# LayerNorm scaling with gamma in PSUM, and five gate operations moved from VectorE to GpSimd

## The chip, the cores and the metric

The kernel runs on one core of a Trainium2 chip. The metric is device time in microseconds (us) of one execution; lower is better. Engines are named as in the profile: PE (TensorE matmul), PEld (its weight loads), DVE (VectorE), ACT (ScalarE), POOL (GpSimd), SP (SyncE, which here only issues transfers). Line numbers such as L331 are those of the kernel before the change; the changed file numbers the same statements two or three higher.

## The reference

The program is two layers on images x of shape 32 x 128 x 56 x 56, all in fp32. Only the first layer's normalisation and gating matter here:

```python
x = depthwise_conv_7x7(input) + dw_bias            # 32 images, 128 channels, 56 x 56
x = transpose(x, (0, 2, 3, 1))                     # tokens: T = 32*56*56 = 100352, C = 128
x = (x - mean(x)) / sqrt(var(x) + 1e-6) * ln_gamma + ln_beta
logits = x @ Wg + bg                               # E = 8 experts
topv, topi = top_k(logits, 2)
wts = softmax(topv)                                # w0, w1
order = argsort(-wts[:, 0])                        # tokens by priority, for the experts' capacity
# each expert keeps its first CAP = 1.25*T/8 tokens: gelu(x@W1+b1)@W2+b2, weighted by wts
out = input + x_skip + layer_scale * moe_out
```

The second layer (coordinate attention and a 3 x 3 convolution) follows and is not touched.

## The kernel before

The program runs in stages, one after the other in time: the depthwise convolution (0 to 600 us), the LayerNorm and gating stage (600 to 1095), the routing, that is, the search for each expert's threshold (from 1093), the experts (to 3120) and the second layer (to the end). A scheduling layer orders the instructions of each engine when the program is built; on the chip each engine then goes through its list in order, and waits on semaphores.

The LayerNorm stage takes two images at a time, a pair, as 49 tokens on each of 128 partitions, and a pair in two units of 24 and 25 tokens per partition (`halves`). For each unit:

- `centre` (L293): SP loads the pair's channels into `lnyt` (two tiles). PE multiplies each token column by `proj`, which subtracts the mean and also forms the eight logits (L310), into PSUM tiles of three tokens each (`lnp`, eight tiles). ACT copies them to `cen` (L311, four tiles) and squares them for the variance: for the first unit of a pair ACT sums as well (L315), for the second it leaves squares in `sqs` (L317).
- `spread` (L319): for the second unit DVE sums the squares (L322). POOL turns sums into variances (L323) and raises them to the power -1/2 (L324), giving `rstd`.
- `normalise` (L326): DVE scales each token with one instruction (L331): `cen` times its `rstd`, times gamma, which lies in SBUF as `gamma_bc`, on all partitions. The result goes into `row`, the pair's tile `xn` of 49 rows of 137 numbers (128 channels, 8 gates, one number for the later expert). Two such tiles exist (`xp`, bufs 2). L333 scales the logits.
- Once a pair: `top` (L234) finds the two largest logits with a chain of dependent DVE operations on 392 elements (49 tokens x 8 experts), leaving one-hot masks `oh0` and `oh1`. `exp` (L254) runs on ACT. `gates` (L257) forms the weights w0 and w1 and from them five arrays of 392 elements, then SP sends the row tile to `acc_d` in DRAM with one transfer of 3356.5 KB (L276).

The stages are pipelined: the loop at L337 centres unit k, normalises unit k-2, and runs `top` or `gates` for pair (k-3)//2. In the built order a pair's `gates` stand on DVE between the scalings of the first and the second unit of the next pair, directly behind the sum L322. The order there is: 24 scalings (the first of which needs the row tile of the pair two before to have reached DRAM), L333, L261, L270, L262, L322, L263, a scaling, L264, a scaling, L265, L267, L268, a scaling, L269, L272, a scaling, L274, the other 21 scalings, L333, then `top` of the same pair, and the first scaling of the next pair just before the last mask of `top` (L248).

`prio` (L274) holds each token's priority for each chosen expert. Routing reads it with its first count (L447). POOL's queue holds in this stage L323 and L324 for each unit; behind the stage come its memset of `zr` (L628), which starts a zero fill of part of `acc_d` that ACT issues (L631), and the scaling of the experts' weights (L722).

Of the kernel before, what the change touches and what calls it, by code (L numbers as in the profile page):

```python
# [8 lines left out]
F32 = mybir.dt.float32  # L9
# [4 lines left out]
ALU = mybir.AluOpType  # L14
AX = mybir.AxisListType
PSUM = bass.MemoryType.PSUM
DRAM = bass.MemoryType.DRAM

N, C, H, W = 32, 128, 56, 56
HW = H * W  # L20
T = N * HW
E = 8
CAP = int(1.25 * T / E)
FF = 4 * C
P = 128
NT = T // P
NPAIR = N // 2
TPP = 2 * HW // P
# [14 lines left out]
def bc(ap, shape):  # L43
    return ap.to_broadcast(shape)
# [3 lines left out]
def moe_conv_then_coordatt_kernel(ctx: ExitStack, tc: tile.TileContext, a: dict, out: bass.AP):  # L48
    nc = tc.nc
# [14 lines left out]
    def load(name, shape, src, eng=None):  # L64
        t = const.tile(list(shape), F32, name=name)
        (eng or nc.sync).dma_start(t, src)
        return t
# [12 lines left out]
    gamma_bc = load("gamma_bc", [P, C], a["ln_gamma"].rearrange("c x -> x c").partition_broadcast(P))  # L80
# [20 lines left out]
    with ExitStack() as st:  # L101
# [3 lines left out]
        pp = st.enter_context(tc.tile_pool(name="dwp", bufs=8, space=PSUM))  # L105
# [44 lines left out]
        for q in range(NQ_):  # L150
# [6 lines left out]
            for i, (t0, offsets, least) in enumerate(PRODUCTS):  # L157
# [14 lines left out]
                for r in range(QC):  # L172
                    c = QC * q + r
                    if i == 0:
                        k = (c % 2) * (C // 2) + c // 2
# [15 lines left out]
    prio = prp.tile([P, E, NT], F32, name="prio")  # L191


    with ExitStack() as st:
# [2 lines left out]
        qp = st.enter_context(tc.tile_pool(name="lnq", bufs=1, reuse_waits="tile"))  # L197
        xp = st.enter_context(tc.tile_pool(name="lnx", bufs=2, reuse_waits="tile"))
        sp = st.enter_context(tc.tile_pool(name="lns", bufs=3, reuse_waits="tile"))
        pp = st.enter_context(tc.tile_pool(name="lnp", bufs=8, space=PSUM))  # L200
        halves = ((0, TPP // 2), (TPP // 2, TPP))
        U = TPP - TPP // 2
        NSQ = TPP // 2
# [11 lines left out]
        def over_tokens(x, n):  # L215
            return bc(x.unsqueeze(1), [P, n, E])

        def over_experts(x, n):
            return bc(x.unsqueeze(2), [P, n, E])

        class Pair:
# [2 lines left out]
            def __init__(self, i):  # L224
                self.i = i

            def tile(self, pool, tag, shape=None):
                return pool.tile(shape or [P, TPP], F32, tag=tag, name=f"{tag}{self.i}", bufs=2 if pool is xp else 1)

            def open(self):  # L230
                self.row = self.tile(xp, "xn", [P, TPP, RW])
# [2 lines left out]
            def top(self):  # L234

                l, n = self.l, TPP
                nc.vector.tensor_tensor(l, l, over_tokens(logit_c, n), ALU.add)
                t = self.tile(sp, "gt", [P, TPP, E])
                self.oh = [self.tile(sp, f"oh{k}", [P, TPP, E]) for k in range(2)]
                self.m = [self.tile(sp, f"m{k}") for k in range(2)]  # L240
                self.later, second = self.tile(sp, "later"), self.tile(sp, "second")
                for k in range(2):
                    nc.vector.tensor_reduce(self.m[k], l, AX.X, ALU.max)
                    nc.vector.tensor_tensor(t, l, over_experts(self.m[k], n), ALU.is_equal)
                    nc.vector.tensor_tensor(t, t, over_tokens(rank_e, n), ALU.mult)
                    mx = (self.later, second)[k]
                    nc.vector.tensor_reduce(mx, t, AX.X, ALU.max)
                    nc.vector.tensor_tensor(self.oh[k], over_tokens(rank_e, n), over_experts(mx, n), ALU.is_equal)  # L248
                    if k == 0:
                        nc.vector.scalar_tensor_tensor(l, self.oh[0], -3.0e38, l, ALU.mult, ALU.add)  # L250
                nc.vector.tensor_tensor(self.m[1], self.m[1], self.m[0], ALU.subtract)
                nc.vector.tensor_tensor(self.later, self.later, second, ALU.min)
# [3 lines left out]

            def gates(self):  # L257

                n, mx, w0, w1 = TPP, self.m[1], self.tile(sp, "w0"), self.tile(sp, "w1")
                t = self.tile(sp, "gt", [P, TPP, E])  # L260
                nc.vector.tensor_tensor(mx, mx, one_t, ALU.min)  # L261
                nc.vector.tensor_tensor(w0, mx, one_t, ALU.add)  # L262
                nc.vector.reciprocal(w0, w0)  # L263
                nc.vector.scalar_tensor_tensor(w0, w0, 0.5, one_t, ALU.max, ALU.min)  # L264
                nc.vector.tensor_tensor(w1, mx, w0, ALU.mult)  # L265
                row, oh = self.row, self.oh
                nc.vector.tensor_tensor(row[:, :, C : C + E], oh[0], over_experts(w0, n), ALU.mult)  # L267
                nc.vector.tensor_tensor(t, oh[1], over_experts(w1, n), ALU.mult)  # L268
                nc.vector.tensor_tensor(row[:, :, C : C + E], row[:, :, C : C + E], t, ALU.add)  # L269
                nc.vector.scalar_tensor_tensor(row[:, :, C + E : RW], self.later.unsqueeze(2), -1.0, all_e.unsqueeze(2),  # L270
                                               ALU.mult, ALU.add)
                nc.vector.tensor_tensor(oh[1], oh[0], oh[1], ALU.add)  # L272
                cols = slice(self.i * TPP, (self.i + 1) * TPP)
                nc.vector.tensor_tensor(prio[:, :, cols].rearrange("p e t -> p t e"), oh[1], over_experts(w0, n), ALU.mult)  # L274
                rows = slice(self.i * TPP * P, (self.i + 1) * TPP * P)
                nc.sync.dma_start(acc_d[rows, :].rearrange("(p j) c -> p j c", p=P), row)  # L276

# [2 lines left out]
        class Unit:  # L280
# [45 lines left out]
            def normalise(self):  # L326
                pair = pairs[self.i]
                if self.h == 0:
                    pair.open()
                for j in range(self.n):  # L330
                    nc.vector.scalar_tensor_tensor(pair.row[:, self.j0 + j, 0:C], self.cen[:, j, 0:C],  # L331
                                                   self.rstd[:, j : j + 1], gamma_bc, ALU.mult, ALU.mult)
                nc.vector.tensor_tensor(pair.l[:, self.j0 : self.j1, :], self.cen[:, :, C : C + E],  # L333
                                        over_experts(self.rstd, self.n), ALU.mult)

# [16 lines left out]
    with ExitStack() as st:  # L352
        rc = st.enter_context(tc.tile_pool(name="rc", bufs=1, reuse_waits="tile"))
        sp = st.enter_context(tc.tile_pool(name="rts", bufs=2, reuse_waits="tile"))
# [243 lines left out]
        xp = st.enter_context(tc.tile_pool(name="fx", bufs=1, reuse_waits="tile"))  # L598
# [30 lines left out]
        for k in range(4):  # L629
            r0, n = T1 + k * T // 4, T // 4 // P // BLK  # L630
# [227 lines left out]
    with ExitStack() as st:  # L858
        cp1 = st.enter_context(tc.tile_pool(name="cc", bufs=1, reuse_waits="tile"))
        xp = st.enter_context(tc.tile_pool(name="cx", bufs=2, reuse_waits="tile"))  # L860
        kp = st.enter_context(tc.tile_pool(name="ck", bufs=3, reuse_waits="tile"))
        sp = st.enter_context(tc.tile_pool(name="cs", bufs=2, reuse_waits="tile"))
# [23 lines left out]
        w0, w1, w2 = (wc[:, k] for k in range(3))  # L886
# [51 lines left out]
        for k in range(2):  # L938
            t = cp1.tile([C, H + 2, W + 2], F32, name=f"pad{k}")
# [196 lines left out]
```

## Time and profile before

| | us |
|---|---|
| median of three runs | 4329.18 |
| lowest and highest | 4310.08, 4334.66 |
| the profiled execution | 4323.54 |
| its span on the core | 4321.8 |
| DVE busy, of the span | 2571.0 (59%) |
| POOL busy, of the span | 2752.9 (64%) |
| PE busy, of the span | 3526.6 (82%) |
| L331, 784 scalings, busy | 213.5 |

The shares are averages over stages that differ; a stage is read from its own stretch. A line of the timeline gives the start (us from the span's start), the time that it took, engine, line, operation, out<-in, shapes, the number of instructions merged, and in brackets idle time in front and what ended it. DVE's records overlap: the next instruction starts up to some 0.1 us before the last has ended, so the cost of one is read from start to start. A line of a group gives after the bar the busy time in us and the mean duration of one in ns, and after the second bar the idle time in front. A line of the waits gives who waited for whom: us in total, times, the longest.

### The profile page before, as it was taken

Reading aid. Unit: us, or ns where it says so; the run is one execution under the profiler, and the core shown is the slowest. Engines: PE = TensorE matmul, PEld = TensorE weight load, DVE = VectorE, ACT = ScalarE, POOL = GpSimd, SP = SyncE. Lnnn points to the kernel's source line nnn. Section 1 sums busy time; section 2 is a strip of 40 time slices with the busy share of each in tenths; the row PEclk is TensorE's granted clock in tenths of the full one; section 3 lists DMA queues with packets and bytes.
Section 4 is the critical chain, followed back from the end, with each engine's and each line's share of the span. In section 5 each row is a group of like instructions: output and inputs, shape, how many; then the busy total and the mean of one; then the engine's idle time right before and its main releaser. Section 6 shows DMA issues by size and latency. Waiting matters only on the chain. (4 is left out here: it accounts for less than half of the span.)

```text
span 4321.8 us, 60777 instructions
## 1 busy us (share of the span) xinstructions
PE 3526.6 (82%) x21765; PEld 2018.7 (47%) x21765; DVE 2571.0 (59%) x5370; ACT 1447.6 (33%) x3123; POOL 2752.9 (64%) x2044
## 2 busy tenths in 40 slices
PE   7999979884169858778688668989669999999999
PEld 4555559884134434444344334434334444454444
DVE  4333329999748648775622112222268888888886
ACT  0000027664034424334344334545312333333332
POOL 5444414333057777576777467777779877788875
PEclk9999989786579879889799889999879999999999
DMA  9999985553982121111222122222265555555551
GB/s 183 179 186 191 188 179 222 245 239 166 327 267 51 51 61 43 48 44 49 54 56 56 45 59 57 56 56 57 60 226 163 193 182 176 166 192 182 184 163 73
DMA packets 678005, 580.92 MB, mean 134 GB/s; under 512 B 405848, under 2 KB 611184, under 8 KB 667248
## 3 DMA queue, kind: packets, MB, share of 16 engines
q1 hardware_dynamic: 411408, 319.81, 25.7%
q10 hardware_dynamic: 222816, 160.70, 14.1%
q0 software_dynamic: 43264, 94.64, 8.1%
q8 instruction: 187, 3.06, 0.3%
q14 instruction: 330, 2.70, 0.2%
HBM read 314.92 MB, written 260.09 MB: 133 GB/s over the span
## 5 line engine op out<-in xcount | busy, mean ns | idle before, releaser
L702 POOL DMA_INDIRECT acc_d<-yo,row x676 | 685.7, 1014 | 274.9 <-DMA acc_d<-yo,row 70.4
L1041 PE MATMUL pc<-v,wk 128*128 128x392 f32 x1920 | 705.5, 510 | 0.4 <-POOL v L1026 0.4
L661 PE MATMUL ph<-fxt,w 128*128 128x512 f32 (+1 forms) x1400 | 682.5, 631 | 0.5 <-ACT ht L662 0.5
L640 POOL DMA_INDIRECT xg_r<-acc_d,idx x556 | 557.4, 1003 | 183.9 <-issue 108.5
L669 PE MATMUL py<-ht,w 128*128 128x512 f32 (+1 forms) x1400 | 624.6, 589 | 0.0
L165 PE MATMUL acc<-xs,band 28*64 28x432 f32 (+2 forms) x11264 | 536.1, 527 | 51.8 <-issue 33.0
L662 ACT ACTIVATE ht<-ph,bias 128x512 f32<-128x512 f32 (+1 forms) x700 | 476.8, 682 | 248.9 <-PE ph L661 246.4
L1041 PEld LDWEIGHTS pc<-v,wk 128*128 128x128 f32 x1920 | 348.2, 191 | 308.5 <-issue 104.9
L165 PEld LDWEIGHTS acc<-xs,band 28*64 28x64 f32 x11264 | 311.2, 132 | 276.1 <-issue 182.9
L310 PE MATMUL lnps<-proj,lnyt 128*128 128x136 f32 x1568 | 364.7, 401 | 67.4 <-ACT sq L315 38.8
L661 PEld LDWEIGHTS ph<-fxt,w 128*128 128x128 f32 x1400 | 274.1, 207 | 279.3 <-issue 250.9
L310 PEld LDWEIGHTS lnps<-proj,lnyt 128*128 128x128 f32 x1568 | 350.9, 316 | 81.7 <-ACT sq L315 47.9
L669 PEld LDWEIGHTS py<-ht,w 128*128 128x128 f32 x1400 | 254.6, 190 | 261.1 <-issue 259.2
L1051 DVE SCALAR_TENSOR_TENSOR y<-pc,y 128x392 f32<-128x392 f32 x640 | 317.3, 553 | 14.9 <-PE pc L1041 14.9
L1021 POOL TENSOR_TENSOR d<-pad 128x3248 f32<-128x3248 f32 x32 | 228.0, 7125 | 151.8 <-DVE pad L1013 151.8
L958 POOL TENSOR_TENSOR cxn<-cxn,cx 128x896 f32<-128x896 f32 x112 | 267.3, 2395 | 75.6 <-DMA cxn<-acc_d 28.8
L696 DVE TENSOR_TENSOR ys<-pb,xg_r 128x512 f32<-128x512 f32 (+2 forms) x147 | 98.3, 671 | 341.3 <-PE pb L678 341.1
L181 DVE TENSOR_TENSOR yt<-acc,m 128x448 f32<-128x448 f32 x256 | 146.4, 620 | 260.3 <-PE acc L165 188.3
L671 ACT ACTIVATE fyt<-py,b 128x512 f32<-128x512 f32 (+1 forms) x175 | 119.6, 683 | 507.0 <-PE py L669 496.7
L653 DVE COPY fxt<-pt 128x512 f32<-128x512 f32 (+1 forms) x175 | 119.5, 683 | 241.7 <-PE pt L651 238.7
L693 ACT ACTIVATE yo<-xg_r,own 128x137 f32<-128x137 f32 (+1 forms) x568 | 194.3, 404 | 191.1 <-DVE own L689 128.3
L331 DVE SCALAR_TENSOR_TENSOR xn<-cen,rstd,gamma_bc 128x128 f32<-128x128 f32 x784 | 213.5, 340 | 47.2 <-POOL rstd L324 47.2
(243 smaller groups left out, 5035.4 us busy)
## 6 DMA issues: line engine op xcount, KB each, us to landing
acc_d<-xn SPq DMA_DIRECT2D x16, 3356.5 KB
acc_d<-yo ACTq DMA_DIRECT2D x4, 13426.0 KB
lnyt<-y_d SPq DMA_DIRECT2D x16, 3136.0 KB
x<-in_x SPq DMA_DIRECT2D x16, 3136.0 KB
cxn<-acc_d SPq DMA_DIRECT2D x112, 448.0 KB
cx<-acc_d SPq DMA_DIRECT2D x112, 448.0 KB
out<-y ACTq DMA_DIRECT2D x64, 784.0 KB
xt<-in_x ACTq DMA_DIRECT2D x64, 392.0 KB
```

The source lines that it names most:

```text
L165: nc.tensor.matmul(acc[r][half * M : (half + 1) * M, :, lo:hi], lhsT=band[rows, t0 + o - least, 1 - par : 1 - par + M], rhs=xs[i][rows, ha ...
L310: nc.tensor.matmul(ps[:, j, :], lhsT=yf[:, self.j0 + g + j, :], rhs=proj, start=True, stop=True)
L331: nc.vector.scalar_tensor_tensor(pair.row[:, self.j0 + j, 0:C], self.cen[:, j, 0:C], self.rstd[:, j : j + 1], gamma_bc, ALU.mult, ALU.mult)
L640: d = nc.gpsimd.indirect_dma_start(out=xg[0:n, k, :], out_offset=None, in_=acc_d[0:T1, :], in_offset=bass.IndirectOffsetOnAxis(ap=idx[0][0 ...
L661: nc.tensor.matmul(ph[:, 0:N_], lhsT=w[0][:, f * P : (f + 1) * P], rhs=xt[:, 0:N_], start=True, stop=True)
L662: nc.scalar.activation(ht[:, f, 0:N_], ph[:, 0:N_], AF.Gelu, bias=w[2][:, f : f + 1])
L669: nc.tensor.matmul(py[:, 0:N_], lhsT=w2[:, f, :], rhs=ht[:, f, 0:N_], start=(f == 0), stop=(f == NF - 1))
L702: d = nc.gpsimd.indirect_dma_start(out=acc_d[:, :], out_offset=bass.IndirectOffsetOnAxis(ap=row[0:n, k : k + 1], axis=0), in_=yo[0:n, k, : ...
L958: nc.gpsimd.tensor_tensor(xn, xn, x2, ALU.add)
L1021: nc.gpsimd.tensor_tensor(d, high, low, ALU.subtract)
L1041: nc.tensor.matmul(m[k], lhsT=wk[k][:, dw, :], rhs=v[:, k, rows, dw : dw + W], start=(dw == 0), stop=(dw == 2))
L1051: nc.vector.scalar_tensor_tensor(r[x], m[k], f, r[y_], ALU.mult, ALU.add)
```

## The change

Gamma is copied once into a PSUM tile, and the scaling reads it there. For it the PSUM pool of the products has seven tiles instead of eight. In `gates`, five operations on 392 elements are issued on POOL instead of DVE: the two products with w0 and w1 (L267, L268), their sum into the row (L269), the sum of the masks (L272) and the product for `prio` (L274). They work in place in the masks, without the tile `gt`, in a new order, and the masks and the weights have two tiles each.

```diff
-        pp = st.enter_context(tc.tile_pool(name="lnp", bufs=8, space=PSUM))
+        pp = st.enter_context(tc.tile_pool(name="lnp", bufs=7, space=PSUM))
+        gp = st.enter_context(tc.tile_pool(name="lng", bufs=1, space=PSUM))
+        gamma_ps = gp.tile([P, C], F32, name="gamma_ps")
+        nc.vector.tensor_copy(gamma_ps, gamma_bc)
...
-                self.oh = [self.tile(sp, f"oh{k}", [P, TPP, E]) for k in range(2)]
+                self.oh = [self.tile(sp, f"oh{k}", [P, TPP, E], 2) for k in range(2)]
...
-                n, mx, w0, w1 = TPP, self.m[1], self.tile(sp, "w0"), self.tile(sp, "w1")
-                t = self.tile(sp, "gt", [P, TPP, E])
+                n, mx, w0, w1 = TPP, self.m[1], self.tile(sp, "w0", None, 2), self.tile(sp, "w1", None, 2)
...
-                nc.vector.tensor_tensor(row[:, :, C : C + E], oh[0], over_experts(w0, n), ALU.mult)
-                nc.vector.tensor_tensor(t, oh[1], over_experts(w1, n), ALU.mult)
-                nc.vector.tensor_tensor(row[:, :, C : C + E], row[:, :, C : C + E], t, ALU.add)
                 nc.vector.scalar_tensor_tensor(row[:, :, C + E : RW], self.later.unsqueeze(2), -1.0, all_e.unsqueeze(2),
                                                ALU.mult, ALU.add)
-                nc.vector.tensor_tensor(oh[1], oh[0], oh[1], ALU.add)
+                nc.gpsimd.tensor_tensor(row[:, :, C : C + E], oh[0], over_experts(w0, n), ALU.mult)
+                nc.gpsimd.tensor_tensor(oh[0], oh[0], oh[1], ALU.add)
                 cols = slice(self.i * TPP, (self.i + 1) * TPP)
-                nc.vector.tensor_tensor(prio[:, :, cols].rearrange("p e t -> p t e"), oh[1], over_experts(w0, n), ALU.mult)
+                nc.gpsimd.tensor_tensor(prio[:, :, cols].rearrange("p e t -> p t e"), oh[0], over_experts(w0, n), ALU.mult)
+                nc.gpsimd.tensor_tensor(oh[1], oh[1], over_experts(w1, n), ALU.mult)
+                nc.gpsimd.tensor_tensor(row[:, :, C : C + E], row[:, :, C : C + E], oh[1], ALU.add)
...
-                                                   self.rstd[:, j : j + 1], gamma_bc, ALU.mult, ALU.mult)
+                                                   self.rstd[:, j : j + 1], gamma_ps, ALU.mult, ALU.mult)
```

More of the change, by code (lines that the diff above doesn't have):

```diff
@@ L225, in __init__, with tile @@
                 self.i = i
-            def tile(self, pool, tag, shape=None):
-                return pool.tile(shape or [P, TPP], F32, tag=tag, name=f"{tag}{self.i}", bufs=2 if pool is xp else 1)
+            def tile(self, pool, tag, shape=None, bufs=1):
+                return pool.tile(shape or [P, TPP], F32, tag=tag, name=f"{tag}{self.i}", bufs=2 if pool is xp else bufs)
             def open(self):
```

## The prediction

> **What bounds the kernel now.** I read the page's engine slices first (the change sits in slices 7 to 10, 600 to 1095 us), then the busy time by stretch. In the stretch 700 to 1000 us, columns after the window are PE, PEld, DVE, ACT, POOL busy time, granted clock, DMA share, GB/s:
>
> ```profile
> 650.00:700.00 50.00, 50.00 (x229) 50.00 (x229) 44.39 (x130) 40.22 (x182) 22.54 (x9) 1.00 0.50 197
> 700.00:1000.00 300.00, 258.39 (x1097) 246.13 (x1097) 296.35 (x845) 200.55 (x831) 118.50 (x45) 0.83 0.60 243
> ```
> ```profile
> ACT cen L311 <- DVE lgs L333: 92.2, 21, 6.9
> ```
>
> DVE works 296 of 300 us. PE leads only in the start-up (50 of 50 us), and the list of waits (third line) has ACT waiting for DVE. So a pair of images costs what DVE spends on it, which the DVE timeline shows:
>
> ```profile
> 814.54 0.34 DVE L331 SCALAR_TENSOR_TENSOR xn<-cen,rstd,gamma_bc 128x128 f32<-128x128 f32 x1
> ...
> 822.07 3.48 DVE L322 TENSOR_REDUCE var<-sqs 128x25 f32<-128x3200 f32 x1
> 825.46 0.46 DVE L263 RECIPROCAL w<-w 128x49 f32<-128x49 f32 x1
> ...
> 827.75 0.55 DVE L269 TENSOR_TENSOR xn<-xn,gt 128x392 f32<-128x392 f32 x1
> ...
> 842.00 0.34 DVE L331 SCALAR_TENSOR_TENSOR xn<-cen,rstd,gamma_bc 128x128 f32<-128x128 f32 x1
> ```
>
> The first scaling of a pair starts at 814.54 and of the next at 842.00: a period of 27.46 us. Call the end of L322 (825.46) the mark. The second thing to see: the first scaling writes a row tile of which there are two, so it must wait until the row of the pair two before is in DRAM. Here are POOL, SP, and the DMA share after the same mark:
>
> ```profile
> 825.64 0.21 POOL L323 TENSOR_SCALAR var<-var 128x25 f32<-128x25 f32 x1 [13.00 <-DVE var L322]
> 825.94 4.31 POOL L324 TENSOR_TENSOR rstd<-var,mhalf 128x25 f32<-128x25 f32 x1
> ```
> ```profile
> 828.33 0.33 SPq L276 DMA_DIRECT2D acc_d<-xn  x1
> 837.27 0.36 SPq L298 DMA_DIRECT2D lnyt<-y_d  x1
> ```
> ```profile
> 828.30:829.20 0.90, 0.90 (x6) 0.90 (x5) 0.90 (x3) 0.84 (x6) 0.90 (x1) 0.50 0.48 209
> 829.20:837.40 8.20, 7.59 (x35) 7.19 (x33) 8.06 (x27) 5.93 (x28) 4.61 (x3) 0.85 0.93 396
> 837.40:838.30 0.90, 0.90 (x5) 0.90 (x5) 0.87 (x2) 0.90 (x4) 0.90 (x1) 1.00 0.43 74
> ```
>
> The row leaves at 828.33, 0.03 us after L269 ends, and its packets end at 837.33; 842.00 is when its tile is wanted. There are under five microseconds to spare, and no wait shows. POOL spends 4.31 us on a power right behind the mark.
>
> **The change, part by part.**
>
> *Five operations leave DVE.* From start to start L267, L268, L269, L272 take 0.48 us each and L274 0.66: 2.57 us a pair.
>
> *gamma in PSUM.* A scaling of 128 elements takes 0.262 us from start to start now. The nearest row with one PSUM and one SBUF tensor and a per-partition scalar is L966: a 512 and a 384 together take 1.18 us (3921.42 to 3922.60). At 1.04 us per 1000 elements (3136 in 3.33 us at L1012, 392 in 0.47 at L1047) that leaves 0.123 us fixed, so 128 cost 0.257: 49 x 0.005 = 0.2 us a pair less. Bounds: -0.2, and +2.9 if what a per-partition scalar adds from SBUF (0.129 fixed against 0.069 of the 49 elements of L251, which pitch at 0.120) came once more with PSUM, 49 x 0.06; I take -0.2, as L966 is the nearest. [...] The copy into PSUM runs once, while DVE waits 47.2 us for the first rstd; were that cover gone it would be one copy, under 0.3 us.
>
> *Seven PSUM tiles for the products, not eight.* Hidden by ACT's waiting for DVE. In the start-up, where PE leads, three products less in flight (3 x 0.22 us): 0 to 0.7 us, once.
>
> *The five operations join POOL's queue.* In the built order each pair's five stand behind L323 and L324 of the unit just reduced:
>
> ```
> L325 var9_1 [waits DVE]   L326 rstd9_1   L271 xn7   L272 oh07   L274 prio   L275 oh17   L276 xn7
> ```
>
> (numbers of the changed file, two or three higher). So they start not when w0 is ready but when the power ends: 0.18 + 0.22 + 0.08 + 4.31 + 0.08 = 4.87 us after the mark. What is queued behind them is the next unit's L323, which ACT releases 8.3 us after the mark and which is wanted most of a period later: free. Their price comes from POOL's products of two SBUF tensors:
>
> ```profile
> L958 POOL TENSOR_TENSOR cxn<-cxn,cx 128x896 f32<-128x896 f32 x112 | 267.3, 2395 | 75.6 <-DMA cxn<-acc_d 28.8 <-PE pc L1041 18.8 <-issue 14.2
> ...
> L141 POOL TENSOR_TENSOR xs<-xt 128x1792 f32<-128x1792 f32 x32 | 101.5, 3172 | 32.6 <-DMA xt<-in_x 20.8 <-DMA y_d<-yt 11.4 <-POOL band L140 0.3
> ...
> L722 POOL TENSOR_TENSOR w<-w,ls_bc 128x512 f32<-128x512 f32 x8 | 10.2, 1276 | 39.2 <-PE ph L661 15.6 <-DVE ys L696 6.8 <-DVE lo_r L516 6.6
> ```
>
> L958's 896 elements take 2.094 (its median; the mean of 2.395 holds collisions) and L722's 512 take 1.276: 2.13 ns an element, so 392 take 1.02 us. Five, with four gaps of 0.08: 5.4 us. Low: L141's 1.77 ns an element, 0.69 each, 3.8 us. High: strides, as between L1031 (2.03 us) and L1026 (1.65) of one size, a factor of 1.23: 6.6 us.
>
> *The two engines meet.* These rows show a product on POOL and DVE operations with two SBUF inputs excluding each other:
>
> ```profile
> 1086.68 2.66 POOL L722 TENSOR_TENSOR w<-w,ls_bc 128x512 f32<-128x512 f32 x2 [3.92 <-DMA w<-in_W]
> 1086.79 1.27 DVE L262 TENSOR_TENSOR w<-m,one_t 128x49 f32<-128x49 f32 x1
> ```
>
> L262 (0.20 elsewhere) is held until POOL's first product is done. L966 and L1051, with one input in PSUM, keep their pace beside L1021 on POOL (3919 to 3926), so the scalings from PSUM should leave POOL free. They end 7.0 us after the mark: two or three of the five run undisturbed, the others meet top()'s chain. I add 1.0 us to POOL's five (two waits of about 0.5), from 0 to 3.0 (two waits of 1.6, as L323 shows at 1.81 against 0.21), and 2.2 us to DVE's chain (it waits out two products that began first, 1.02 each, and a gap; 0 to 5.1 for five). [...]
>
> *The row leaves later.* From the first scaling of pair p+1 to that of p+2 now runs: 10.92 to the mark, less 24 x 0.005: 10.8; queue and power 4.87; five operations 6.4; SP 0.03; issue to last packet 0.83 + 8.96 (mean of the eleven steady transfers in the trace's packets, 8.16 to 10.03) = 9.79; landing to the waiting engine 0.76 (the first matmul of the stage, 617.58 to 618.34). Sum 32.65 us. The load lnyt, which SP issues right behind, runs after it: lnyt0 and lnyt1, issued 0.45 us apart, moved in turn.
>
> DVE's own work is 27.46 - 2.57 - 0.2 + 2.2 = 26.9 us, inside 32.65. So the saving hides behind a new wait of 5.8 us: DVE's first scaling waits for the DMA. Per pair 32.65 - 27.46 = +5.2 us, for the fourteen pairs 2 to 15: +72.7. Bounds by the five operations (3.8 to 9.6): 30.05 to 35.85, +36 to +117; by the transfer (8.16 to 10.03) another -11 to +15.
>
> *The tail.* After pair 15 starts, DVE saves pair 14's 2.57 and the 1.07 + 0.8 us that L722 held L262 and L614; the last three operations to prio take 3.3 us on POOL against 3.2 now. Routing starts 4.3 us sooner, but the zero fill of acc_d, behind five gates and two L722 in POOL's queue, 0.5 us later. I take -2 (-4.3 to +0.5).
>
> Sum: +71 us. The profiled execution took 4323.54 (span 4321.8 plus 1.7), so 4394; the median of the three runs is 5.6 above it, so 4400.
>
> **The rivals.**
>
> *Faster.* The row still lands in time and DVE's work sets the period: 24.7 us without meeting, -2.76 x 15 - 2 = -43, 4286. It decides once five operations take under 1.2 us (26.25 + 1.2 = 27.46). For it: before has spare time at that wait. Against: 0.24 us each, a third of the lowest row.
>
> *About the same.* Operations at 0.5 us and transfers of 8.2 us: 28.0, +8 us, 4337. No row is that fast.
>
> *POOL starved.* Each of the five is kept out by DVE's chain like L323: 5.4 + 5 x 1.6 = 13.4, period 39.6, +168, 4497; with three of them +115, 4444. Against: the chain's dependent gaps let POOL in.
>
> *PSUM slows the scaling.* At the upper bound, 0.06 us each, 24 of them lie in the loop: +1.5 a pair, +21, 4421. Against: L966.
>
> **How the numbers follow.** The row wait as summed 0.70 (4360 to 4430); PSUM slow on top 0.08; starved 0.11; about the same 0.05; faster 0.06. Range 4352 to 4440, leaving out both ends. 0.5% (22 us) is about what a measurement tells from no change, as the three runs span 25. Faster 0.06, same 0.05, slower 0.89.
>
> **What would show it.** Right: idle time on DVE before the scaling, released by the DMA acc_d<-xn, some 5 us in fourteen places; the row leaving about 11 us after L322's end; POOL's five at about 1 us each; scalings at 0.257 us; DVE busy about 27 of 32.6 us. Wrong: no such wait, or POOL's five ahead of the power, or far under a microsecond.

## The result, and the profile after

The changed kernel takes 4383.64 us (median of six runs, 4372.19 to 4394.32) against 4323.16 before (six runs, 4310.08 to 4334.66): a ratio of 1.0150 with a 95% interval of 1.0129 to 1.0172, so 60 us slower. The forecast was 4400, the range 4352 to 4440. The profiled execution took 4379.09, with a span of 4377.3.

The time lies where it was expected. From the first product of the LayerNorm stage to the first count of the routing it was 474.4 us before and is 528.1 now: +53.7. The rest of the program differs by a few microseconds in both directions: in the profiled executions the stage starts 6.2 us later after the change, and what follows it is 4.2 us shorter.

The busy time of the stretch from 700 to 1000 us, whose columns are those of the same view before (window, its length, PE, PEld, DVE, ACT, POOL, granted clock, DMA share, GB/s):

```profile
700.00:1000.00 300.00, 225.83 (x981) 218.30 (x981) 242.27 (x678) 178.06 (x735) 139.83 (x89) 0.82 0.54 215
```

No engine is full any more. VectorE worked 296 of 300 us before and works 242 now, and nothing else took its place at the top. That is the sign of a wait that everything shares, and the list of waits over the whole stage (who waited for whom: us in total, times, longest) names it in the second line here:

```profile
ACT cen L313 <- DVE lgs L335: 145.4, 12, 13.4
...
DVE xn L333 <- DMA acc_d<-xn: 73.4, 14, 6.3
```

Fourteen waits of 5.2 us in the mean; the line was not there before. ACT's wait for VectorE grew with it (102.9 us in 24 waits before, over the whole stage) and is its echo: in the kernels below that have no such wait it is at 89 to 103 us again. One turn of the loop, on VectorE:

```profile
822.13 0.45 DVE L265 RECIPROCAL w<-w 128x49 f32<-128x49 f32 x1
...
829.13 0.87 DVE L335 TENSOR_TENSOR lgs<-cen,rstd 128x200 f32<-128x200 f32 x1
830.04 1.12 DVE L240 TENSOR_TENSOR lgs<-lgs,logit_c 128x392 f32<-128x392 f32 x1
...
842.52 0.35 DVE L333 SCALAR_TENSOR_TENSOR xn<-cen,rstd,gamma_ps 128x128 f32<-128x128 f32 x1 [5.29 <-DMA acc_d<-xn]
...
853.35 0.45 DVE L265 RECIPROCAL w<-w 128x49 f32<-128x49 f32 x1
```

on POOL:

```profile
822.60 4.31 POOL L326 TENSOR_TENSOR rstd<-var,mhalf 128x25 f32<-128x25 f32 x1
826.87 0.87 POOL L271 TENSOR_TENSOR xn<-oh,w 128x392 f32<-128x392 f32 x1
827.82 1.01 POOL L272 TENSOR_TENSOR oh<-oh,oh 128x392 f32<-128x392 f32 x1
828.91 0.87 POOL L274 TENSOR_TENSOR prio<-oh,w 128x392 f32<-128x392 f32 x1
829.74 0.99 POOL L275 TENSOR_TENSOR oh<-oh,w 128x392 f32<-128x392 f32 x1
830.81 1.20 POOL L276 TENSOR_TENSOR xn<-xn,oh 128x392 f32<-128x392 f32 x1
```

and on SP's queue:

```profile
832.03 0.33 SPq L278 DMA_DIRECT2D acc_d<-xn  x1
834.33 0.36 SPq L300 DMA_DIRECT2D lnyt<-y_d  x1
```

Read them in this order. The reciprocal starts at the mark (822.13, then 853.35: a period of 31.22 us). The power stands ahead of the five operations, the row leaves at 832.03, 9.90 us after the mark (2.87 before), its packets run from 832.87 to 842.06, and the scaling that wants the tile has been standing for 5.29 us when it starts at 842.52. The two lines at 829.13 and 830.04 are operations held by POOL's products: 0.87 and 1.12 us where they take 0.35 and 0.57 otherwise.

### The profile page after: what moved, and what is told of

It reads as the page before. It is cut to its first block, busy times and chain, and to the rows that moved or that the text cites. A ratio compares the mean times of both kernels' runs of the same rounds, so it can differ in the third digit from the quotient of the medians.

```text
span 4377.3 us, 60783 instructions
## 1 busy us (share of the span) xinstructions
PE 3522.8 (80%) x21765; PEld 2026.0 (46%) x21765; DVE 2550.2 (58%) x5291; ACT 1447.5 (33%) x3123; POOL 2803.4 (64%) x2124
## 5 line engine op out<-in xcount | busy, mean ns | idle before, releaser
L165 PE MATMUL acc<-xs,band 28*64 28x432 f32 (+1 forms) x11264 | 536.0, 528 | 58.3 <-issue 41.2
L1053 DVE SCALAR_TENSOR_TENSOR y<-pc,y 128x392 f32<-128x392 f32 x640 | 317.4, 554 | 11.2 <-PE pc L1043 11.2
L333 DVE SCALAR_TENSOR_TENSOR xn<-cen,rstd,gamma_ps 128x128 f32<-128x128 f32 x784 | 208.5, 339 | 120.5 <-DMA acc_d<-xn 73.4
## 6 DMA issues: line engine op xcount, KB each, us to landing
acc_d<-xn SPq DMA_DIRECT2D x16, 3356.5 KB
```

Of the source, the lines that this page charges most:

```text
L165: nc.tensor.matmul(acc[r][half * M : (half + 1) * M, :, lo:hi], lhsT=band[rows, t0 + o - least, 1 - par : 1 - par + M], rhs=xs[i][rows, ha ...
L1053: nc.vector.scalar_tensor_tensor(r[x], m[k], f, r[y_], ALU.mult, ALU.add)
```

## The experiments

Theory: the period is the row tile's loop, and the price is the late row. Rivals: GpSimd and VectorE exclude each other, and that is what is paid; GpSimd's own work; gamma in PSUM.

The scheduling layer answers most edits with another order on VectorE, which would change the loop too. So the kernels below (unless said otherwise) get VectorE's order of the changed kernel by force, with edges that order and need no semaphore:

```diff
+        for x, y in zip(rows, rows[1:]):      # rows: VectorE's instructions in the wanted order
+            tc.add_manual_dep(y.ins, x.ins.name, mybir.DependencyInfo(mybir.DependencyClass.NoSync, ...))
```

In the first four kernels below this list costs 2 us once, between the second and the third mark (24.2 to 24.4 us against 22.2 in the changed kernel).

Eight of the eleven kernels ran on chips on which the kernel before takes 4872 to 4886 us instead of 4323 (the three others, need later with four tiles, load a pair sooner and w1 first, where it takes 4318). No profile of the kernel before was taken there; in the profiles of the edited kernels the LayerNorm stage is as long as their edits alone account for, and the time from the routing to the end is 490 to 570 us longer. So times are compared by their ratio to the kernel before on the same chip, and the expectations, written with the first chip's 4323, are to be read as differences from it. "Period" is the mean of the thirteen intervals between the third and the sixteenth mark; "stage" reaches from the first product to the first count.

| kernel | period, us | stage, us | ratio to before, 95% interval |
|---|---|---|---|
| before | 27.45 | 474.4 | |
| the changed kernel | 31.27 | 528.1 | 1.0150, 1.0129 to 1.0172 |
| gamma alone | 27.26 | 476.9 | 1.0014, 0.9992 to 1.0035 |
| five operations alone | 34.81 | 578.3 | 1.0235, 1.0194 to 1.0276 |
| two operations for prio | 26.22 | 462.2 | 0.9973, 0.9948 to 0.9998 |
| five ahead of the power | 26.92 | 470.9 | 1.0024, 1.0006 to 1.0042 |
| need later | 31.83 | 542.0 | 1.0129, 1.0082 to 1.0175 |
| need later, four tiles | 27.68 | 483.2 | 1.0043, 1.0021 to 1.0065 |
| prio product last | 30.12 | 514.6 | 1.0086, 1.0056 to 1.0116 |
| load later | 31.11 | 528.0 | a single execution |
| load later, a pair sooner | 30.74 | 523.0 | a single execution |
| balanced | 25.31 | 451.3 | 0.9946, 0.9920 to 0.9971 |
| balanced, w1 first | 24.74 | 443.8 | 0.9923, 0.9896 to 0.9951 |

### Gamma alone

```diff
-                self.rstd[:, j : j + 1], gamma_bc, ALU.mult, ALU.mult)
+                self.rstd[:, j : j + 1], gamma_ps, ALU.mult, ALU.mult)
```

with seven PSUM tiles for the products, and the gate operations where they were.

> Gamma in PSUM alone; the five gate operations stay on VectorE, and VectorE's order is held as it was before. Theory (the row leaves late and VectorE waits for it): nothing in this part touches the row, so no wait for the transfer; a scaling every 0.258 us instead of 0.262 is 0.2 us a pair, about -3 us in all, 4320, no difference that can be measured. Rival (a scaling from PSUM is dearer): up to +0.06 us each, 49 a pair with VectorE the bound, +2.9 us a pair, +44 us, 4367.

The period is 27.26 us, 0.19 less than before; the forecast's term was 0.2. VectorE's timeline of this kernel:

```profile
822.89 6.02 DVE L341 SCALAR_TENSOR_TENSOR xn<-cen,rstd,gamma_ps 128x128 f32<-128x128 f32 x23
```

23 scalings from 822.89 to the next instruction at 828.83 are 0.258 us each, where one with gamma in SBUF took 0.262: PSUM is no dearer here. What the part does cost is the start-up: the first mark comes 0.9 us later and the interval from it to the second is 1.3 us longer (18.3 against 17.0). The kernel with eight PSUM tiles (the next one) does not show these 2.2 us, and all with seven do.

### The five operations alone

```diff
+                nc.gpsimd.tensor_tensor(...)          # the five, as in the change
-                self.rstd[:, j : j + 1], gamma_ps, ALU.mult, ALU.mult)
+                self.rstd[:, j : j + 1], gamma_bc, ALU.mult, ALU.mult)
```

> The five operations on GpSimd alone; gamma stays in SBUF, and VectorE's order is held as in the changed kernel. Theory: the row still leaves behind the power and the five operations, so the wait is there, and longer: the scalings that run beside the five now read two SBUF tensors and keep GpSimd out, up to the 1.6 us for each that L323 showed at its worst, and are held by it in turn. The period goes from 31.2 us to between 32 and 39; I take 34, +39 us against the changed kernel, about 4423. Rival (where gamma lies does not matter to GpSimd): the five take 5.1 us as in the changed kernel, period 31.2 to 31.4, 4384 to 4387.

34.81 us: the theory's number (34), not the rival's (31.2). POOL's timeline and VectorE's:

```profile
840.18 3.44 POOL L273 TENSOR_TENSOR xn<-oh,w 128x392 f32<-128x392 f32 x1
843.70 1.23 POOL L274 TENSOR_TENSOR oh<-oh,oh 128x392 f32<-128x392 f32 x1
```
```profile
837.81 4.80 DVE L336 SCALAR_TENSOR_TENSOR xn<-cen,rstd,gamma_bc 128x128 f32<-128x128 f32 x18
842.54 0.35 DVE L338 TENSOR_TENSOR lgs<-cen,rstd 128x200 f32<-128x200 f32 x1
842.92 1.12 DVE L239 TENSOR_TENSOR lgs<-lgs,logit_c 128x392 f32<-128x392 f32 x1
...
859.16 0.35 DVE L336 SCALAR_TENSOR_TENSOR xn<-cen,rstd,gamma_bc 128x128 f32<-128x128 f32 x1 [7.78 <-DMA acc_d<-xn]
```

The first product takes 3.44 us instead of 0.87: it ends at 843.62, 0.7 us after the train of scalings and the scaling of the logits behind it (842.89), while the scalings keep their pace (4.73 us for 18, 0.263 each). So a train of operations with two SBUF inputs kept GpSimd out almost until it ended. The kernel before has it too, on a shorter operation: the variance L323, 0.21 us otherwise, takes 1.81 us from 833.75 and ends at 835.56, just behind the logits' scaling that closes VectorE's train (835.49). So gamma in PSUM is worth 3.5 us a pair (34.81 against 31.27) to the five operations, as they stand; both parts of the change belong together.

### Two operations for prio

```diff
                 nc.vector ... row = oh0*w0; gt = oh1*w1; row += gt     # as before
-                nc.vector.tensor_tensor(oh[1], oh[0], oh[1], ALU.add)
+                nc.gpsimd.tensor_tensor(oh[1], oh[0], oh[1], ALU.add)
-                nc.vector.tensor_tensor(prio..., oh[1], over_experts(w0, n), ALU.mult)
+                nc.gpsimd.tensor_tensor(prio..., oh[1], over_experts(w0, n), ALU.mult)
```

> Gamma in PSUM; of the five, only the sum of the masks and the product for prio go to GpSimd, the three that the row needs stay on VectorE, whose order is else held. Theory: the row leaves 2.9 us after the mark again, and row tile's loop is 10.8 + 2.9 + 0.8 + 9.0 to 10.0 + 0.5 = 24 to 25 us; VectorE's own work is 27.46 - 0.2 - 1.14 = 26.1 us and sets the period: -1.3 us a pair, about -20 us, 4303, and no wait for the transfer. Rival (the engines exclude each other, so that what VectorE is spared comes back as holding): two operations of 1 us hold VectorE for up to 2 us, period 26.1 to 28.1, 4303 to 4333, in the main no change.

The period is 26.22 (forecast 26.1), and no wait for the transfer remains. The stretch from 700 to 1000 us, and POOL:

```profile
700.00:1000.00 300.00, 263.12 (x1142) 254.13 (x1142) 295.08 (x861) 210.47 (x876) 129.87 (x72) 0.88 0.64 259
```
```profile
837.05 1.02 POOL L281 TENSOR_TENSOR oh<-oh,oh 128x392 f32<-128x392 f32 x1
838.15 0.88 POOL L283 TENSOR_TENSOR prio<-oh,w 128x392 f32<-128x392 f32 x1
```

VectorE is full again (295 of 300 us) and saves 1.04 of the 1.14 us against gamma alone (27.26), beside two products of GpSimd that meet only scalings from PSUM. At most 0.1 us came back as holding. The ratio, 0.9973, is less than the -20 us expected, 0.9954: the thirteen periods are 16.0 us shorter, but the start-up is 4.7 us longer (PSUM tiles and list), and the stage is left with 12.2.

### The five ahead of the power

```diff
+        behind = [(units[2 * q + 5].up, pairs[q].last) for q in range(NPAIR - 2)]   # variance behind the fifth
```

> The changed kernel with the five operations ahead of the power (and the variance) of the unit just reduced in GpSimd's queue; VectorE's order is held. Theory: the five start when w0 is ready, about 1.0 us after the mark instead of 4.7; the row leaves 3.7 us sooner, and the loop is 31.2 - 3.7 = 27.5 us (up to 28.3 with the slower transfers), so the wait falls from some 5.5 us to 1 to 2, and the time to about that of before: 4323 to 4335. Rival (contention of GpSimd and VectorE is what the changed kernel pays): the same five operations meet the same engine, period 31.2, 4384.

```profile
832.50 0.87 POOL L276 TENSOR_TENSOR xn<-oh,w 128x392 f32<-128x392 f32 x1 [13.35 <-DVE w L271]
...
836.32 0.99 POOL L281 TENSOR_TENSOR xn<-xn,oh 128x392 f32<-128x392 f32 x1
...
837.69 4.32 POOL L331 TENSOR_TENSOR rstd<-var,mhalf 128x25 f32<-128x25 f32 x1
```
```profile
832.59 0.84 DVE L272 TENSOR_TENSOR w<-m,w 128x49 f32<-128x49 f32 x1
...
847.70 0.35 DVE L339 SCALAR_TENSOR_TENSOR xn<-cen,rstd,gamma_ps 128x128 f32<-128x128 f32 x1 [1.45 <-DMA acc_d<-xn]
```

The same instructions in another order on one queue, and the wait falls from 5.2 us in the mean to 1.5 and the period by 4.35 us, to less than the 27.5 expected. The rival of contention, which had 31.2, is out as the cause of the period. (The ratio, 1.0024, is some 15 us above what the stage's -3.5 us would give; the difference lies outside this stage and its cause is open.)

### The need later, and what took the wait's place

```diff
-  24 scalings of the first unit, their logits, the sum of squares (mark), w, 25 scalings of the second
+  12 scalings of the first unit, the sum of squares (mark), w, the other 12, their logits, 25 scalings of the second
```

This is VectorE's list before and after. 12 scalings are moved, one fewer than the expectation counts.

> The changed kernel, GpSimd's order untouched (power first, then the five); on VectorE 13 of the 24 scalings of a pair's first unit, with the scaling of its logits, stand behind the next mark instead of ahead of it. The row leaves as late as in the changed kernel, but between the first scaling, which wants the tile, and the mark lie 13 scalings fewer. Theory: the loop shrinks by 13 x 0.258 + 0.27 = 3.6 us, from 31.2 to 27.6 (28.5 where the transfer is slow), unless ACT, which now gets its tile of centred tokens back later, leads: 4.3 + 18.4 + 3.5 + 0.3 = 26.5. So 27.6 to 28.5, -3 to -3.6 us a pair against the changed kernel, and +2 to +20 us against the kernel before. Rival (the two engines' contention, or GpSimd's own work, is what the changed kernel pays): VectorE and GpSimd do the same operations, period 31.2.

The theory's number failed: the period is 31.83 us, nearest to the rival's 31.2. But the trace shows another reason. POOL's timeline:

```profile
846.96 4.31 POOL L331 TENSOR_TENSOR rstd<-var,mhalf 128x25 f32<-128x25 f32 x1 [3.72 <-DVE lgs L341]
```

The power, at once behind the variance in the changed kernel, stood 3.72 us. Its result has three tiles, so it writes the one of three units before, and the last to read that is the scaling of the logits, which the edit had put behind the mark. What the loop won on VectorE it lost on POOL. With a fourth tile:

```diff
-                self.rstd = self.tile(sp, "rstd")
+                self.rstd = sp.tile([P, U], F32, tag="rstd", name=f"rstd{self.nm}", bufs=4)[:, 0 : self.n]
```

> As the run with the need moved later, with four tiles for the power's result instead of three. In that run the power waited 3.7 us in each pair for the scaling of the logits that had been moved behind the mark, which still read the tile that the power was to write. Theory: with a fourth tile that wait is gone, the power starts 0.4 us after the mark again, and the loop is 7.6 (first scaling to mark, as measured) + 4.7 + 5.1 to 5.5 + 0.9 + 9.1 + 0.5 = 27.9 to 28.3 us, about -3.3 us a pair against the changed kernel, +10 us against the one before. Rival (something else holds the period at 31 to 32 us, as contention or GpSimd's work): no change, 31.8 us.

```profile
867.30 4.31 POOL L331 TENSOR_TENSOR rstd<-var,mhalf 128x25 f32<-128x25 f32 x1
```
```profile
859.36 0.35 DVE L339 SCALAR_TENSOR_TENSOR xn<-cen,rstd,gamma_ps 128x128 f32<-128x128 f32 x1 [1.88 <-DMA acc_d<-xn]
```

27.68 us, 0.2 below the sum: the wait on POOL is gone, and the row, which leaves almost as late as in the changed kernel (9.57 us after the mark, 9.91 there), is simply wanted later. The agreement is closer than its terms: the five took 4.8 us instead of 5.1 to 5.5 and the transfer 8.7 instead of 9.1, while in four of the thirteen turns the scaling started 2.1 us after the row's last packet instead of 0.6, for a cause that stays open. GpSimd does here all that it does there, so its work is no bound.

### The product for prio last

```diff
                 nc.gpsimd ... row = oh0*w0; oh0 += oh1
-                nc.gpsimd ... prio = oh0*w0
                 nc.gpsimd ... oh1 *= w1; row += oh1
+                nc.gpsimd ... prio = oh0*w0
```

> The changed kernel with the product for prio behind the row's last sum in GpSimd's queue; VectorE's order is held. Nothing is added or taken away; the row leaves one product sooner. Theory: that product (0.87 us and a gap) leaves the loop, 31.2 - 0.95 = 30.3 us a pair, -13 us against the changed kernel, +42 against the one before. Rival (GpSimd's total work or contention sets the period): no change, 31.2 us.

30.12 us, 1.15 less (0.95 expected). The product, moved out of the loop and still done, took its own time (0.87 us and a gap) off the period; the 0.2 us more is the holding by VectorE, which now falls on the product for `prio` (1.20 us) and no longer on the row's sum (0.99, and 1.20 in the changed kernel).

### The load behind the row

In the changed kernel the load of the next images is issued 2.3 us behind the row (834.33), on the same queue; before, it was 8.9 us behind, about when a transfer of 8.2 us had ended.

```diff
+            tc.add_manual_dep(units[2 * q].load.ins, pairs[q - 1].v[0][0].ins.name, ... Sync ...)   # first scaling
```

> The changed kernel, but the load of the next images waits until the first scaling, and with it the row's landing, is past, so that the row's transfer has nothing queued behind it. Theory: the mean packet falls back from 1.08 us to the 1.005 us of the kernel before and the transfer from 9.1 to 8.8 us, 0.3 us a pair; the images still land some 14 us before they are wanted. Rival (the transfer is slower for another reason): packets stay at 1.08 us and the period at 31.2 to 31.4 us.

The edge pointed at a scaling one pair too late: TensorE now waited for the images (13 times, up to 11.2 us), so this period says nothing on the theory, as the list of waits shows:

```profile
PE lnps L317 <- DMA lnyt<-y_d: 115.8, 13, 11.2
```

The packets do: 1.008 us in the mean instead of 1.08, and 8.45 us in the mean for a row instead of 9.1. With the edge a pair sooner (`pairs[q - 2]`):

> The changed kernel with the load of the next images behind the landing of the row that it follows in the queue, now a pair sooner than in the run before, so that TensorE does not wait for it. Theory: packets at 1.01 us, the transfer at 8.4 us as in the run before instead of 9.1 to 9.5, period 31.2 - 0.8 = 30.4 us, no wait of TensorE for the images. Rival (the transfer's time does not reach the period): 31.2 us.

The list of waits has no wait for the images any more, and VectorE's timeline shows the row's wait a microsecond shorter:

```profile
838.57 0.35 DVE L339 SCALAR_TENSOR_TENSOR xn<-cen,rstd,gamma_ps 128x128 f32<-128x128 f32 x1 [4.33 <-DMA acc_d<-xn]
```

Eight of the thirteen periods are 30.23 to 30.29 us (30.4 expected; 31.22 to 31.24 is the usual one of the changed kernel), two are 32.1, where the transfer took 10.0 us instead of 8.2 with nothing queued behind it. So the load behind the row costs 1.0 us in an undisturbed turn and 0.5 in the mean, and the transfers of 10.0 us, which the kernel before had too, have a cause that stays open. The changed kernel shows the price of the load by itself: behind its last rows no load is queued, and there the packets take 1.004 to 1.008 us, a row 8.15 to 8.41, and the last two periods are 30.53 and 30.24 us.

### A version that is faster than both

The three moves that each shortened the loop, together: the five ahead of the power, the product for prio last, six scalings behind the mark (the expectation says seven).

```diff
-  VectorE: 24 scalings of the first unit, their logits, the sum of squares (mark), w, 25 scalings of the second
+  VectorE: 18 scalings of the first unit, the sum of squares (mark), w, the other 6, their logits, 25 of the second
-  GpSimd: variance, power; row = oh0*w0; oh0 += oh1; prio = oh0*w0; oh1 *= w1; row += oh1
+  GpSimd: row = oh0*w0; oh0 += oh1; oh1 *= w1; row += oh1; prio = oh0*w0; variance, power
```

> Gamma in PSUM and all five on GpSimd, with three moves that keep the row out of the way: the five ahead of the power, the product for prio last of them, and 7 of the first unit's 24 scalings behind the next mark. Theory: the row's loop is 31.2 - 4.3 (as gates first showed) - 0.95 - 7 x 0.258 - 0.27 = 23.9 us, ACT's loop about 3.0 + 18.4 + 3.5 + 0.3 = 25.2, and VectorE's own work 27.46 - 2.57 - 0.2 + 0.64 = 25.3; so 25.3 us a pair, no wait for the transfer, -2.1 us x 14 = -30 us and +1 in the start-up: 29 us faster than before, and faster than the two operations alone (26.2 us a pair). Rival (what VectorE is spared comes back as holding by GpSimd's products): five products, up to 1 us each, 26 to 27.5 us a pair, -20 to 0 us.

25.31 us for each pair with no wait for the transfer, as worked out from VectorE's own 24.69 us (27.26 of gamma alone less 2.57) and one operation that is held. VectorE and POOL:

```profile
870.51 0.84 DVE L272 TENSOR_TENSOR w<-m,w 128x49 f32<-128x49 f32 x1
```
```profile
870.42 0.87 POOL L276 TENSOR_TENSOR xn<-oh,w 128x392 f32<-128x392 f32 x1 [4.70 <-DVE w L271]
```

The first product began 0.09 us before the product for w1 and held it for 0.64 us. So the last kernel lets w1 go first:

```diff
+                tc.add_manual_dep(self.first.ins, W[4].ins.name, ... Sync ...)     # the first of the five behind w1
```

> The balanced kernel with GpSimd's first product behind VectorE's product for w1, which that product held for 0.64 us in each pair. Theory: w1 takes 0.2 us again and the period is VectorE's own 24.7 us, -0.64 us a pair and -9 us against the balanced kernel, about 38 us faster than before. Rival (the meeting moves to the next operation of VectorE with two SBUF inputs, the scaling of the logits or the first of the search): 25.3 us, no change; or ACT's loop, worked out at 25.2 us, leads: 25.2 us.

```profile
862.27 0.20 DVE L272 TENSOR_TENSOR w<-m,w 128x49 f32<-128x49 f32 x1
```
```profile
700.00:1000.00 300.00, 274.55 (x1191) 265.01 (x1192) 294.82 (x870) 209.93 (x916) 165.56 (x108) 0.89 0.63 260
```

Twelve of the thirteen periods are 24.66 to 24.68 us: VectorE's own work and nothing else (295 of 300 us busy). Neither rival holds: the meeting did not move on to another operation, and ACT's loop does not lead at 25.2. The thirteenth is 25.65, with a wait of 0.9 us for a row whose transfer took 9.9 us, so under a microsecond is left to spare. The ratio is 0.9923 (0.9896 to 0.9951): 33 us faster than before, 98 faster than the changed kernel by the two ratios. The stage gives 30.6 of them; it loses 2.7 in the start-up and 2.0 behind the last mark, where the moved scalings come late.

## Why the prediction was right, point by point

The bound, the mechanism and the place were right: VectorE before, then the row tile's loop, in fourteen places. The total came nearer to the forecast than the terms did, and that is in part luck: +71 us were forecast and 60 measured, of which the stage gives 53.7; the rest lies outside it, where nothing was forecast. The loop's terms, as forecast and as the turn ending at 853.35 has them:

| term | forecast, us | measured, us |
|---|---|---|
| first scaling to mark | 10.8 | 10.83 |
| queue and power | 4.87 | 4.74 |
| the five operations | 6.4 | 5.14 |
| SP | 0.03 | 0.02 |
| issue to last packet | 9.79 | 10.03 |
| landing to the waiting engine | 0.76 | 0.46 |
| sum | 32.65 | 31.22 |

- *The five operations* were the mis-sized term, by 1.26 us. The price scaled from products of 512 and 896 elements (1.02 us and a gap, 5.4 for five) was 0.6 high: undisturbed, ahead of the power, the five take 4.8 us. The meeting, put at 1.0, was 0.3 on POOL's side. On VectorE's side it was 1.1 us (829.13 to 831.19 is 2.06 us, against 0.98 without POOL) where 2.2 were allowed.
- *The landing* was taken from TensorE's wait for images (0.76 us) and is shorter on VectorE (0.46).
- *The transfer* was right for a wrong reason. The prediction had the load run after the row. It does start only as the row ends (841.45 in the trace's packets), yet the row's packets are slower with it queued behind (1.10 us against 1.005), and taking it away gave 1.0 us.
- *The new wait*: 5.8 forecast, 5.2 measured. *Per pair*: +5.2 forecast, +3.8 measured, thirteen times 49.6 us; behind the last mark +1.4, which is 2.8 in the fourteenth turn, up to its first scaling, less 1.4 from there to the count (2 forecast); and the start-up, forecast at 0 to 0.7, takes 2.7, of which gamma alone, with its seven tiles, shows 2.2. Sum 53.7, as the stage shows.
- *The rivals.* "PSUM slows the scaling" is refuted by gamma alone (0.258 us a scaling). "POOL starved" is what the five alone would have been, and 3.5 us a pair, not 8: GpSimd loses 2.6 us to a train of operations once, at its first product, and 0.2 to 0.3 at each of the others. The rival's own sum for three starved operations is off: 26.25 + 5.4 + 3 x 1.6 = 36.5 us a pair makes +124, not +115. "Faster" needed the row to land in time; the balanced kernels show that it is there to be had, by order and not by faster operations, which the rival's condition (five operations in under 1.2 us) had missed.

## What to carry to other kernels

When work moves to an idle engine, look at what it stands behind in that engine's queue and who waits for its result: here 4.3 us of a power and 5.1 us of products came between the first weights and a transfer that had under five microseconds to spare. Before giving such a change up, take the loop that it lengthened and try its terms one by one: order on the receiving queue, what needs to be done before the transfer at all, and when the buffer is next wanted. A buffer that is released later has its own readers and writers: here the scaling of the logits, moved behind the mark, kept the power waiting for 3.7 us until the power's result was given a fourth tile.

## What the runs showed of the hardware

- A train of VectorE operations with two SBUF inputs made a GpSimd product take 2.6 us longer (3.44 us against 0.87, the five alone), until 0.7 us after the train's end, and was not slowed itself (0.263 us each). A single such operation that started 0.09 us after a GpSimd product was held until that ended (the product for w1 in the balanced kernel, 0.84 us against 0.20).
- GpSimd's power, 4.47 us with two SBUF inputs, held none of them: the search of the two largest logits kept its 0.60 us pace beside it (832.59 to 837 in the changed kernel).
- The same transfer of 3356.5 KB takes 8.2 us alone (8.16 to 8.21 in eight of the sixteen rows of the kernel before), about 9.2 with a load queued 2.3 us behind it (the changed kernel), and now and then 10.0 with nothing queued (two of the thirteen turns with the load a pair sooner).
- Periods worked out from the first chip's profile were met to 0.2 us (27.26 for gamma alone, 26.22, 25.31) on chips on which the kernel before takes 13% longer (4872 to 4886 us against 4323): in the profiles taken there this stage is as long as the edits account for, and the time from the routing to the end is longer, by 490 to 570 us.
